# Attention with shared diagonal score blocks: pairs of diagonal blocks in 192 columns, and x loaded in quarters

## The chip, the cores and the metric

The kernel runs on one core of one Trainium2 chip. A core has a matrix engine (PE, with its weight loads shown apart as PEld), a vector engine (DVE), a scalar engine (ACT), GpSimd (POOL), a queue engine (SP) that here only issues DMAs, an on-chip memory (SBUF)[...]. The metric is device time in microseconds of one execution, as the median of several runs.

## The reference

For each of 32 images with 256 channels and 1024 positions, the input is normalised in groups of eight channels, projected to queries, keys and values of eight heads of 32 channels, and each position attends to the positions strictly before it. Position 0 has no such position and receives 0. The input is added to the result.

```python
xf = _gn(x).reshape(B, C, S)                    # 32 groups of 8 channels
q = jnp.einsum('oc,bcs->bos', q_w, xf) + q_b[None, :, None]
kv = jnp.einsum('oc,bcs->bos', kv_w, xf) + kv_b[None, :, None]
k, v = (kv[:, :EMBED_C], kv[:, EMBED_C:])       # then q, k, v to 8 heads
mask = jnp.tril(jnp.ones((S, S), dtype=x.dtype), -1)
scores = jnp.einsum('bhqd,bhkd->bhqk', q, k) / jnp.sqrt(dk)
attn = jax.nn.softmax(jnp.where(mask == 0, -10000.0, scores), axis=-1)
attn = jnp.where(mask == 0, 0.0, attn)
out = x + jnp.einsum('bhqk,bhkd->bhqd', attn, v)   # back to B, C, H, W
```

## The kernel before

All is float32. The 256 channels are two groups `g` of 128 partitions, each with four heads of 32 partitions; the 1024 positions are two halves `hf` of 512 queries and eight key blocks `kb` of 128. Scores are computed transposed, with keys on partitions and queries along the columns. Only the blocks on and below the diagonal are computed, 36 blocks of 128x128 for each head.

**Pieces and visits.** A `piece` is what one key block gives to one half of the queries: 512 columns, or 256 (a half piece). Pieces of which a part lies above the diagonal are filled up: the second diagonal key block of a half has 384 columns and takes the last 128 from the fourth. For each group there are six visits of one full and one half piece, and so twelve visits in a batch element (called a batch here). The list `visits` says which pieces are scored together, and `products` which are then multiplied by the values.

**A visit.** The main loop does, in this order for visit i: `scores(i)`; then what hangs on `at[i]` (one unit of the projections of the next batch, the issue of loads, `stack`, `invert`); then `values(i-1)`, the products of the visit before; then what hangs on `after[i]` (normalisation steps, `fold`, `sum_folded`, `finish`). [...] The places of the hooks within the twelve visits are the lists `PROJECT`, `PREPARE`, `SUMS` and `FINISH`.

- `scores` (L285): each product has 32 rows (one head) and 64 keys, so that four heads and two halves of a key block occupy different parts of the PE array. The half pieces of heads 2 and 3 come first, then the full piece of heads 0 to 3, then, after a wait on the semaphore `bank_free`, the half pieces of heads 0 and 1, which share their banks with those of heads 2 and 3. Three exponentials on ACT follow: two of the full piece (L348, tile `e`) and one of the half piece (L346, tile `eh`). A full float32 product stands in the trace as two passes.
- `mask` (L301): a select on POOL sets the part of diagonal blocks above the diagonal to 0, in place in `e` or `eh`.
- `values` (L373): products of 128 keys and 32 channels for each head, into one accumulator bank per half. At the last one ACT copies the bank to `num` (L386). An addition on DVE (L381) sums the exponentials of a half over its key blocks, into the tile of its first piece (tag `e0`).
- The denominators: `fold` adds the 128 partitions of that sum onto 32 by two accumulating DMAs from POOL's queue (L397, with a drain before the second one for n=1), `stack` moves them by SP, `sum_folded` (L410, L411), `invert` and two DMAs bring the inverses back as `rb`.
- `finish` (L483, L484): `num` times `rb`, plus the bias of v, plus x; then the output DMA.
- Normalisation of a later batch: `norm_channels` (statistics on DVE, L168), `norm_mean` (a product `pm` on PE, L158), `norm_deviation` (three small DVE steps `dev`, L186 to L188), `norm_variance` (a product `pv` on PE, which reads `dev`), `norm_rstd` (POOL), `norm_apply` (ACT, L224, tile `xn`). `pm` is at the end of visit 3 and `pv` at the end of visit 4 of the batch before.
- Projections (L158 through `product`): q and k in 512 columns, v in 256, from `xn`.
- `load` (L107): two DMAs of 512 KB for a batch, in visit 6.

In the last batch some of the key sums are made by PE (`sums`, L418) in place of the additions, and the inverses by DVE alone (`invert_here`).

Of the kernel before, what the change touches and what calls it, by code (L numbers as in the profile page):

```python
# [17 lines left out]
P = 128  # L18
# [10 lines left out]
WIDE = 64  # L29
# [3 lines left out]
def tile_norm_attention_residual(  # L33
# [65 lines left out]
    def unshifted():  # L99
# [3 lines left out]

        def load(b):
            live["x", b] = xpool.tile([P, NG, S], F32, tag="x", name=f"x_{b}")
            for g in range(NG):
                nc.sync.dma_start(out=live["x", b][:, g, :], in_=x_in[b, :, g, :])  # L107
# [16 lines left out]
        def load_weights():  # L124
            for n, w in enumerate((q_w, kv_w[0:C], kv_w[C : 2 * C])):
                live["wn", n] = epool.tile([P, 4, HALFBANK], F32, tag="eh", bufs=4, name=f"wn_{n}")[:, :NG, :C]
                nc.sync.dma_start(out=live["wn", n], in_=w.rearrange("(o p) c -> p o c", p=P))
            nc.sync.dma_start(out=qk_bias[:, 0, :], in_=q_b.rearrange("(g p) -> p g", p=P))
            nc.sync.dma_start(out=qk_bias[:, 1, :], in_=kv_b[0:C].rearrange("(g p) -> p g", p=P))
            nc.sync.dma_start(out=v_bias_col, in_=kv_b[C : 2 * C].rearrange("(g p) -> p g", p=P))  # L130
# [30 lines left out]


# [49 lines left out]
        def norm_apply(b, hf, g):  # L212

            if (hf, g) == (0, 0):
                live["xn", b] = work.tile([P, NG, S], F32, tag="xn", name=f"xn_{b}")
            cols = slice(hf * HALF, (hf + 1) * HALF)
            xn, xt = live["xn", b][:, g, cols], live["x", b][:, g, cols]
            rstd = live["rstd", b][:, g : g + 1]
            if (b, hf, g) == (0, 0, 1):
                nc.scalar.activation(xn, live["less_mean"], AF.Identity, scale=rstd)  # L220
            elif b == 0:
                nc.vector.tensor_scalar(xn, xt, live["minus_mean", b][:, g : g + 1], rstd, ALU.add, ALU.mult)
            else:
                nc.scalar.activation(xn, xt, AF.Identity, bias=live["shift", b][:, g : g + 1], scale=rstd)  # L224

        def project_qk(b, g, n, hf):
# [6 lines left out]
            for cc in range(NG):  # L233
                product(
                    pp, wT[:, cc, n * C + g * P : n * C + (g + 1) * P], live["xn", b][:, cc, cols],
# [6 lines left out]
        def project_v(b, n):  # L242
# [4 lines left out]
            pp = spare(f"ppv_{b}_{n}").rearrange("p (s c) -> p s c", c=C)  # L247
            for s in range(2):
                for cc in range(NG):
                    product(  # L250
                        pp[:, s, :], live["xn", b][:, cc, (2 * n + s) * P : (2 * n + s + 1) * P],
                        wT[:, cc, 2 * C : 3 * C], start=cc == 0, stop=cc == NG - 1,
                    )
# [12 lines left out]
        def piece(g, hf, k, part=None):  # L266
            d = k - hf * BPH
            if d == 1:

                blocks = [(k, slice(P, HALF), slice(P, HALF)), (k + 2, slice(0, P), slice(3 * P, HALF))]  # L270
            elif d == 2:
                blocks = [(k, slice(0, HALFBANK), slice(HALFBANK, HALF))]
            elif part is not None:
                blocks = [(k, slice(0, HALFBANK), slice(part * HALFBANK, (part + 1) * HALFBANK))]
            else:
                blocks = [(k, slice(0, HALF), slice(0, HALF))]
            return g, hf, k, part, tuple(blocks)

        def scores_of(pc, pair, j, n=0):

            b, (g, hf, k, part, blocks) = pc
            rows = slice(HD * j, HD * (j + 1))
            kb, cols, of = blocks[n]
            return [
                nc.tensor.matmul(  # L285
                    pair[c : c + WIDE, cols], lhsT=live["k", b, g][rows, kb * P + c : kb * P + c + WIDE],
                    rhs=live["q", b, g][rows, hf * HALF + of.start : hf * HALF + of.stop],
                    start=True, stop=True, skip_group_check=True,
                )
                for c in range(0, P, WIDE)  # L290
            ]

        def mask(pc, e, heads=slice(0, 4)):


            g, hf, k, part, blocks = pc
            if k < hf * BPH:
                return
            n = len(blocks)
            diagonal = e[:, heads, : n * P].rearrange("p j (n q) -> p j n q", q=P)  # L300
            nc.gpsimd.affine_select(  # L301
                out=diagonal, in_=diagonal, pattern=[[0, heads.stop - heads.start], [0, n], [1, P]],
                compare_op=ALU.is_gt, fill=0.0, base=0, channel_multiplier=-1,
            )
            if k == 0:
                nc.gpsimd.memset(e[0:1, heads, 0:1], 1.0)

        def scores(b, full, half):


            tag = "e0" if full[2] == 0 else "e"
            name = f"{b}_{full[0]}_{full[1]}_{full[2]}"
            e = epool.tile([P, 4, HALF], F32, tag=tag, bufs=4 if tag == "e0" else 3, name=f"{tag}_{name}")
            eh = epool.tile([P, 4, HALFBANK], F32, tag="eh", bufs=4, name=f"eh_{name}")
            pairs = [ps_s.tile([P, 2, HALF], F32, tag="sT", name=f"sT_{name}_{a}") for a in range(3)]
            short = pairs[2].rearrange("p bank (n q) -> p bank n q", n=2)
            last = b == B - 1 and full[:2] == (NG - 1, NH - 1) and half[2] == NB - 2
            short_of = lambda heads, n: [m for j in heads for m in scores_of((b, half), short[:, j % 2, n, :], j)]
            long_of = lambda heads, n: [scores_of((b, full), pairs[j // 2][:, j % 2, :], j, n) for j in heads]


            if not last:
                first = short_of((2, 3), 1)
                for n in range(len(full[4])):
                    long_of(range(4), n)
            else:

                long_of(range(4), 0)
                long_of((0, 1), 1)
                first = short_of((2, 3), 1)  # L330
                long_of((2, 3), 1)

            for ins in first:
                ins.then_inc(bank_free, 1)
                tc.no_tile_sem_insts.add(ins.ins.name)
            live["free"] = live.get("free", 0) + len(first)
# [3 lines left out]
            for j in range(2):  # L340
                for lo in scores_of((b, half), short[:, j, 0, :], j):
                    for ins in first:
                        tc.declare_no_dep(lo.ins, ins.ins, reason="the semaphore orders them")
            for a in range(3):
                if a == 2:
                    exp = nc.scalar.activation(eh.rearrange("p (n bank) q -> p bank n q", n=2), short, AF.Exp)  # L346
                else:
                    nc.scalar.activation(e[:, 2 * a : 2 * a + 2, :], pairs[a], AF.Exp)  # L348
# [6 lines left out]
            for heads in (range(2), range(2, 4)) if last else (range(4),):  # L355
                mask(full, e, slice(heads.start, heads.stop))
            mask(half, eh)
            live["e", b, full], live["e", b, half] = e, eh

        def values(b, pc, summed=True):  # L360
            g, hf, k, part, blocks = pc
            first, last = k == 0, k == hf * BPH + (1 if hf == 0 else 2)
            e = live.pop(("e", b, pc))
            if not summed:
                live["e", pc] = e
            if first:
                live["acc"] = ps_o.tile([P, HALF], F32, tag="acc", name=f"acc_{b}_{g}_{hf}")
                live["sum", b, g, hf] = e
            acc = live["acc"]
            for kb, cols, of in blocks:  # L370
                for j in range(4):
# [3 lines left out]
                        rhs=e[:, j, cols], start=first, stop=last, skip_group_check=True,  # L375
                    )
                if not summed:
                    continue
                if not first:
                    total = live["sum", b, g, hf]  # L380
                    nc.vector.tensor_add(total[:, :, of], total[:, :, of], e[:, :, cols])  # L381
            if last and (b, g, hf) == (B - 1, NG - 1, NH - 1):
                live["num", b, NH * g + hf] = acc
            elif last:
                num = work.tile([P, HALF], F32, tag="num", bufs=8, name=f"num_{b}_{g}_{hf}")
                nc.scalar.copy(num, acc)  # L386
                live["num", b, NH * g + hf] = num
# [28 lines left out]
        def sum_keys(pd, e, cols, of, start=True, stop=True):  # L416
            for j in range(4):
                nc.tensor.matmul(  # L418
                    pd[HD * j : HD * (j + 1), of], lhsT=pick, rhs=e[:, j, cols],
# [3 lines left out]
        def sums(n, pcs, more=True):  # L423
# [4 lines left out]
            for k, e in enumerate(pcs):  # L428
                if e is None:
                    e, blocks = live.pop(("sum", B - 1, *divmod(n, NH))), ((None, slice(0, HALF), slice(0, HALF)),)  # L430
                else:
                    e, blocks = live.pop(("e", e)) if ("e", e) in live else live["e", B - 1, e], e[4]
                for kb, cols, of in blocks:
# [371 lines left out]
```

## Time and profile before

| | us |
|---|---|
| median of 3 runs (1822.09 to 1822.13) | 1822.12 |
| the profiled execution | 1821.87 |
| its span | 1820.1 |
| PE busy | 1807.9 |
| DVE busy | 1655.6 |
| ACT busy | 1480.0 |
| POOL busy | 798.9 |

The profile is one execution. Its span runs from the first to the last instruction; the profiled execution's own time lies 1.8 us above it. Busy time is the union of an engine's instructions, so overlapping matmuls are counted once; it says how much an engine had to do, and not which wait decided. For that the timeline is read stage by stage. Lines such as L285 are those of the kernel before.

### The profile page before, as it was taken

The page shows a single profiled execution, that of the slowest core. Times are in us where ns is not written, and L with a number is a line of the kernel's source. Part 1 is how long each engine was busy: PE and PEld are TensorE (multiplying, and loading weights), DVE is VectorE, ACT ScalarE, POOL GpSimd, SP SyncE. Part 2 cuts the span into 40 slices and gives each one's busy share as a digit, 9 for nine tenths or more (in the row PEclk, how much of TensorE's full clock was granted, in tenths as well). Part 3 has the DMA queues.
Part 4 walks back from the last instruction along what each step waited for, and adds up shares of the span by engine and source line. Part 5 has one row for each costly group of instructions (what it writes and reads, how often), then busy time and mean ns, then how long its engine had stood idle before and what let it go on. Part 6 is the DMA issues. An engine that isn't in the chain of part 4 may idle for free. (4 is left out here: it accounts for less than half of the span.)

```text
span 1820.1 us, 68098 instructions
## 1 busy us (share of the span) xinstructions
PE 1807.9 (99%) x30388; PEld 837.4 (46%) x30388; DVE 1655.6 (91%) x1762; ACT 1480.0 (81%) x1860; POOL 798.9 (44%) x774
## 2 busy tenths in 40 slices
PE   9999999999999999999999999999999999999997
PEld 5444444444444444444444444444444444444443
DVE  4799999999999999999999999999999999999988
ACT  6888878888888888788887888877888878888885
POOL 1444544535435445344354353443444544435532
PEclk9999999999999999999999999999999999999999
DMA  3457676676776766767767667676667676676662
GB/s 123 71 98 137 134 150 113 133 148 125 147 127 125 143 128 137 148 121 133 142 129 147 116 135 150 124 141 136 123 137 136 134 152 115 129 152 124 124 124 73
DMA packets 77836, 235.91 MB, mean 130 GB/s; under 512 B 20320, under 2 KB 21344, under 8 KB 61664
## 3 DMA queue, kind: packets, MB, share of 16 engines
q0 software_dynamic: 15872, 97.53, 40.1%
q1 hardware_dynamic: 61664, 133.96, 26.4%
q8 instruction: 239, 3.92, 0.9%
q14 instruction: 61, 0.50, 0.1%
HBM read 66.85 MB, written 34.57 MB: 56 GB/s over the span
## 5 line engine op out<-in xcount | busy, mean ns | idle before, releaser
L348 ACT ACTIVATE e<-sT 128x1024 f32<-128x1024 f32 x768 | 745.2, 1022 | 269.3 <-PE sT L285 214.5
L381 DVE TENSOR_TENSOR e<-e,e 128x1536 f32<-128x1536 f32 x376 | 632.5, 1682 | 17.7
L381 DVE TENSOR_TENSOR e<-e,eh 128x1024 f32<-128x1024 f32 x380 | 524.2, 1394 | 112.3 <-PE acc L373 92.8
L301 POOL TENSOR_SCALAR_AFFINE_SELECT e<-e 128x512 f32<-128x512 f32 (+1 forms) x257 | 381.9, 1486 | 549.6 <-ACT e L348 546.4
L285 PE MATMUL sT<-q,k 32*64 32x256 f32 (+3 forms) x14336 | 601.3, 447 | 0.2
L158 PE MATMUL pp<-xn,wT 128*32 128x512 f32 x4096 | 492.4, 598 | 0.1
L285 PEld LDWEIGHTS sT<-q,k 32*64 32x64 f32 x14336 | 353.3, 130 | 212.9 <-ACT eh L346 64.7
L373 PE MATMUL acc<-e,v 128*32 128x512 f32 (+2 forms) x4096 | 400.8, 486 | 0.0
L346 ACT ACTIVATE eh<-sT 128x1024 f32<-128x1024 f32 x384 | 395.6, 1030 | 0.0
L397 POOL DMA_DIRECT2D e<-e x248 | 202.0, 824 | 399.5 <-DMA e<-e 305.3
L158 PE MATMUL ppv<-wT,xn 128*32 128x256 f32 x4096 | 247.5, 382 | 0.0
L373 PEld LDWEIGHTS acc<-e,v 128*32 128x32 f32 x4096 | 133.1, 110 | 223.1 <-issue 192.1
L373 PE MATMUL acc<-eh,v 128*32 128x256 f32 x3072 | 224.6, 379 | 0.0
L158 PEld LDWEIGHTS pp<-xn,wT 128*32 128x32 f32 x4096 | 107.5, 109 | 237.2 <-issue 228.9
L373 PEld LDWEIGHTS acc<-eh,v 128*32 128x32 f32 x3072 | 98.8, 110 | 164.0 <-issue 153.0
L158 PEld LDWEIGHTS ppv<-wT,xn 128*32 128x32 f32 x4096 | 120.3, 109 | 110.8 <-issue 44.7
L301 POOL TENSOR_SCALAR_AFFINE_SELECT eh<-eh 128x512 f32<-128x512 f32 x128 | 166.7, 1302 | 0.6 <-ACT eh L346 0.2
L224 ACT ACTIVATE xn<-x,shift,rstd 128x512 f32<-128x512 f32 x124 | 103.1, 831 | 0.0
L484 DVE SCALAR_TENSOR_TENSOR rb<-rb,v_bias_col,x 128x512 f32<-128x512 f32 x124 | 94.0, 758 | 4.4
L238 ACT ACTIVATE k<-pp,qk_bias 128x512 f32<-128x512 f32 x128 | 89.8, 702 | 2.3 <-PE pp L158 1.2
L238 ACT ACTIVATE q<-pp,qk_bias 128x512 f32<-128x512 f32 x128 | 89.9, 702 | 1.0 <-PE pp L158 1.0
L410 DVE STREAM_TRANSPOSE turned<-folded 128x512 f32<-128x512 f32 x124 | 87.6, 706 | 2.2
(70 smaller groups left out, 665.8 us busy)
## 6 DMA issues: line engine op xcount, KB each, us to landing
e<-e POOLq DMA_DIRECT2D x124, 512.0 KB, 6.8
x<-in_x_dram SPq DMA_DIRECT2D x64, 512.0 KB, 6.3
e<-e POOLq DMA_DIRECT2D x124, 256.0 KB, 4.6
folded<-e SPq DMA_DIRECT2D x124, 256.0 KB, 3.9
rb<-inverses SPq DMA_DIRECT2D x124, 256.0 KB, 8.0
out_dram<-rb SPq DMA_DIRECT2D x124, 256.0 KB, 4.7
inverses<-inv_turned SPq DMA_DIRECT2D x31, 32.0 KB, 1.7
out_dram<-rb_last SPq DMA_DIRECT2D x3, 256.0 KB, 2.5
```

The lines of the kernel that those rows point to most:

```text
L158: nc.tensor.matmul(out[part], lhsT=lhsT[:, part], rhs=rhs, start=start, stop=stop, skip_group_check=True)
L224: nc.scalar.activation(xn, xt, AF.Identity, bias=live["shift", b][:, g : g + 1], scale=rstd)
L238: nc.scalar.activation(live[key][:, cols], pp, AF.Identity, bias=qk_bias[:, n, g : g + 1], scale=(SCALE, 1.0)[n],)
L285: nc.tensor.matmul(pair[c : c + WIDE, cols], lhsT=live["k", b, g][rows, kb * P + c : kb * P + c + WIDE], rhs=live["q", b, g][rows, hf * HA ...
L301: nc.gpsimd.affine_select(out=diagonal, in_=diagonal, pattern=[[0, heads.stop - heads.start], [0, n], [1, P]], compare_op=ALU.is_gt, fill= ...
L346: exp = nc.scalar.activation(eh.rearrange("p (n bank) q -> p bank n q", n=2), short, AF.Exp)
L348: nc.scalar.activation(e[:, 2 * a : 2 * a + 2, :], pairs[a], AF.Exp)
L373: nc.tensor.matmul(acc[HD * j : HD * (j + 1), of], lhsT=live["v", b][:, kb, h * HD : (h + 1) * HD], rhs=e[:, j, cols], start=first, stop=l ...
L381: nc.vector.tensor_add(total[:, :, of], total[:, :, of], e[:, :, cols])
L397: nc.gpsimd.dma_start(out=total[:rows], in_=total[rows : 2 * rows], accum_op=ALU.add)
L410: nc.vector.transpose(turned, live["folded", b][:, j, :])
L484: nc.vector.scalar_tensor_tensor(rb, rb, v_bias_col[:, g : g + 1], xt[:, g, cols], ALU.add, ALU.add)
```

## The change

Two diagonal blocks 2j and 2j+1 were scored in full, 256 columns of 128 keys. Half of each is above the diagonal. The change writes both into 192 columns. It first orders the tokens of each pair of blocks so that the odd block runs backwards (`blocks` with `turned`, when x is normalised into `xn`; `finish` turns the result back). Then the upper 64 keys of the odd block need only its first 64 queries, and so on, and the two blocks' triangles fit beside each other: for the lower 64 partitions 64 columns of the odd block and 128 of the even one, for the upper 64 partitions 128 of the odd and 64 of the even one. `mask` makes the two square blocks of them, each by a select from the raw exponentials in `eh` into a new tile, `diagonal` (kind "D"), one for each half.

The lists of pieces are replaced by tables: `VISITS` (what is scored), `PRODUCTS` (which columns of which tile are multiplied by which values), `ADDS` (which tiles are added into which) and `SUMMED` (the last batch's sums on PE). Four of six visits of a group have a pair beside a long piece of 512 columns (or 384 + 128); two have a half piece of 256. The long pieces now contain only blocks below the diagonal, and need no mask. The sum of the first half is kept in its diagonal tile, that of the second half in the long tile of visit 2. The loads of x become four of 256 KB, in visits 4 to 7. The buffers for `e` go from 3 to 4, for `eh` from 4 to 3, and `xn` is kept in halves with 3 buffers.

```diff
         def norm_apply(b, hf, g):
...
-                nc.scalar.activation(xn, xt, AF.Identity, bias=live["shift", b][:, g : g + 1], scale=rstd)
+            for s in range(2):
+                to, of = blocks(xn, s), blocks(xt, s, s == 1)
+                if b == 0:
+                    nc.vector.tensor_scalar(to, of, live["minus_mean", b][:, g : g + 1], rstd, ALU.add, ALU.mult)
+                else:
+                    nc.scalar.activation(to, of, AF.Identity, bias=live["shift", b][:, g : g + 1], scale=rstd)
...
+        def blocks(tokens, s, turned=False):
+            of = tokens.rearrange("p (n s t) -> p n s t", s=2, t=P)[:, :, s, :]
+            return of[:, :, ::-1] if turned else of
...
+        def pair(j, at):
+            even, odd = 2 * j, 2 * j + 1
+            c0, c1, c2, c3 = (at + n * KEYS for n in range(4))
+            return at, 3 * KEYS, [
+                [
+                    (0, even, even * P, P, slice(c1, c3)),
+                    (0, odd, odd * P, KEYS, slice(c0, c1)),
+                ],
+                [
+                    (KEYS, odd, odd * P, P, slice(c0, c2)),
+                    (KEYS, even, even * P + KEYS, KEYS, slice(c2, c3)),
+                ],
+            ]
...
+        def mask(b, g, raw, j):
+            hf, place = j // 2, (2 * j % 4) * P
+            if ("e", b, g, "D", hf) not in live:
+                live["e", b, g, "D", hf] = epool.tile(
+                    [P, 4, HALF], F32, tag=("e0", "e")[hf], bufs=4, name=f"diagonal_{b}_{g}_{hf}"
+                )
+            square = live["e", b, g, "D", hf]
+            for s in range(2):
+                nc.gpsimd.affine_select(
+                    out=square[:, :, place + s * P : place + (s + 1) * P],
+                    in_=raw[:, :, (1 - s) * KEYS : (3 - s) * KEYS],
+                    pattern=[[0, 4], [(1, -1)[s], P]], compare_op=ALU.is_gt, fill=0.0, base=0,
+                    channel_multiplier=(-1, 1)[s],
+                )
...
         def scores(b, v):
...
+            rest = [lambda: long_of((2, 3), 1)] if len(longs) > 1 else []
+            first = short_of((2, 3))
+            for n in range(len(longs) - 1, -1, -1):
+                long_of((0, 1), n)
+            long_of((2, 3), 0)
...
+            made = short_of((0, 1), *rest if i in PAIRS else ())
...
+        def add_keys(b, v):
+            g, i = divmod(v, len(VISITS))
+            for to, at in ADDS[i]:
+                to = tile_of(b, g, to)
+                nc.vector.tensor_add(to, to, tile_of(b, g, at))
...
         def finish(b, n, within=slice(0, HALF)):
...
-            nc.vector.tensor_mul(rb, num[:, within], rb)
-            nc.vector.scalar_tensor_tensor(rb, rb, v_bias_col[:, g : g + 1], xt[:, g, cols], ALU.add, ALU.add)
+            num = num[:, within]
+            nc.vector.tensor_mul(num, num, rb)
+            for s in range(2):
+                nc.vector.scalar_tensor_tensor(
+                    blocks(rb, s), blocks(num, s, s == 1), v_bias_col[:, g : g + 1], blocks(xt[:, g, cols], s),
+                    ALU.add, ALU.add,
+                )
...
+        VISITS = [
+            ([full(0, P, 3 * P, 0), full(2, 3 * P, P, 3 * P)], [pair(0, 0)]),
+            ([full(1, 2 * P, 4 * P, 0)], [pair(1, 0)]),
+            ([full(0, 4 * P, 4 * P, 0)], [full(1, 6 * P, 2 * P, 0)]),
+            ([full(2, 4 * P, 4 * P, 0)], [pair(3, 0)]),
+            ([full(4, 5 * P, 3 * P, 0), full(6, 7 * P, P, 3 * P)], [full(5, 6 * P, 2 * P, 0)]),
+            ([full(3, 4 * P, 4 * P, 0)], [pair(2, 0)]),
+        ]
+        N, TOTAL = NG * len(VISITS), 2
+        PAIRS = {0: 0, 1: 1, 3: 3, 5: 2}
...
+            (0, [
+                (("L", 0, Q(0, 3)), 0, Q(1, 4)), (("L", 0, Q(3, 4)), 2, Q(3, 4)),
+                (("D", 0, Q(0, 1)), 0, Q(0, 1)), (("D", 0, Q(1, 2)), 1, Q(1, 2)),
+            ]),
+            (0, [(("L", 1, Q(0, 2)), 1, Q(2, 4)), (("D", 0, Q(2, 3)), 2, Q(2, 3)), (("D", 0, Q(3, 4)), 3, Q(3, 4))]),
...
+        ADDS = [
+            [(("L", 0, Q(2, 3)), ("L", 0, Q(3, 4)))],
+            [(("D", 0, Q(1, 4)), ("L", 0, Q(0, 3))), (("D", 0, Q(2, 4)), ("L", 1, Q(0, 2)))],
+            [(("L", 2, Q(0, 2)), ("L", 1, Q(2, 4))), (("L", 2, Q(2, 4)), ("H", 2, Q(0, 2)))],
+            [(("L", 2, Q(0, 4)), ("L", 3, Q(0, 4)))],
+            [
+                (("L", 2, Q(1, 4)), ("L", 4, Q(0, 3))), (("L", 2, Q(3, 4)), ("L", 4, Q(3, 4))),
+                (("L", 2, Q(2, 4)), ("H", 4, Q(0, 2))),
+            ],
+            [(("L", 2, Q(0, 4)), ("D", 1, Q(0, 4))), (("L", 2, Q(0, 4)), ("L", 5, Q(0, 4)))],
+        ]
...
-                    when(max(first - 2 * N + 6, 0), lambda b=b: load(b))
+                    for n in range(NG * NH):
+                        cols = slice(n % NH * HALF, (n % NH + 1) * HALF)
+                        when(max(first - 2 * N + 4 + n, 0), lambda b=b, n=n, cols=cols: load_part(b, n // NH, cols))
```

## The prediction

> **What bounds the kernel now.** I read the page first, for busy shares; then the timeline of one steady batch, PE and DVE apart, because a share of 99% says nothing of where it would give; then the groups by form for durations, and the waits.
>
> The page, part 1:
>
> ```profile
> PE 1807.9 (99%) x30388; PEld 837.4 (46%) x30388; DVE 1655.6 (91%) x1762; ACT 1480.0 (81%) x1860; POOL 798.9 (44%) x774
> ```
>
> TensorE never rests; DVE has 9% left, most of it at the start. A batch is twelve visits (0 to 11). The timeline of PE in visits 4 and 5 (start, length; records overlap, so stages are read start to start):
>
> ```profile
> 654.17 1.93 PE L158 MATMUL ppv<-wT,xn 128*32 128x256 f32 x32
> 655.92 1.04 PE L373 MATMUL acc<-e,v 128*32 128x512 f32 x8
> 656.78 0.61 PE L373 MATMUL acc<-eh,v 128*32 128x256 f32 x8
> 657.27 0.24 PE L158 MATMUL pv<-dev,avg 128*32 128x2 f32 x8
> ...
> 657.44 1.59 PE L285 MATMUL sT<-q,k 32*64 32x256 f32 x48
> 658.96 1.92 PE L158 MATMUL pp<-xn,wT 128*32 128x512 f32 x16
> 660.70 1.04 PE L373 MATMUL acc<-e,v 128*32 128x512 f32 x8
> 661.56 0.61 PE L373 MATMUL acc<-eh,v 128*32 128x256 f32 x8
> 662.10 1.55 PE L285 MATMUL sT<-q,k 32*64 32x256 f32 x32
> 663.58 1.93 PE L158 MATMUL pp<-xn,wT 128*32 128x512 f32 x16
> ```
>
> A visit is scores (662.10 to 663.58, 1.48 us; 1.52 where the long piece is split 384+128), projection (1.74), values (1.40 for 768 columns). Within a score stage the single records put the two passes of a 512-column product 427 ns apart and of a 128-column one 107: 0.83 ns per column and pass, 1.667 per column. So 768 columns are 1.28 of the 1.48 us. DVE over visits 3 and 4:
>
> ```profile
> 649.67 0.69 DVE L483 TENSOR_TENSOR rb<-num,rb 128x512 f32<-128x512 f32 x1
> 650.39 0.75 DVE L484 SCALAR_TENSOR_TENSOR rb<-rb,v_bias_col,x 128x512 f32<-128x512 f32 x1
> 651.18 0.15 DVE L486 COPY rb<-x 128x1 f32<-128x1 f32 x1
> 651.99 2.36 DVE L381 TENSOR_TENSOR e<-e,eh 128x1024 f32<-128x1024 f32 x2 [0.66 <-PE acc L373]
> 654.27 0.68 DVE L483 TENSOR_TENSOR rb<-num,rb 128x512 f32<-128x512 f32 x1
> ...
> 655.66 0.15 DVE L186 TENSOR_TENSOR dev<-mv,mean 128x2 f32<-128x2 f32 x1
> 655.85 0.16 DVE L187 TENSOR_TENSOR dev<-dev 128x2 f32<-128x2 f32 x1
> 656.04 0.54 DVE L188 TENSOR_TENSOR dev<-dev,mv 128x2 f32<-128x2 f32 x1
> ```
>
> The small `dev` ends at 656.58 and the product `pv` on PE that reads it starts at 657.27: 0.69 us to spare, once per batch. That is the narrowest place between the two busiest engines.
>
> Groups by form (busy, mean ns) and one wait:
>
> ```profile
> L381 DVE TENSOR_TENSOR e<-e,eh 128x1024 f32<-128x1024 f32 x380 | 524.2, 1394 | 112.3 <-PE acc L373 92.8 <-POOL e L301 1.6 <-DVE e L381 0.5
> L301 POOL TENSOR_SCALAR_AFFINE_SELECT eh<-eh 128x512 f32<-128x512 f32 x128 | 166.7, 1302 | 0.6 <-ACT eh L346 0.2
> L484 DVE SCALAR_TENSOR_TENSOR rb<-rb,v_bias_col,x 128x512 f32<-128x512 f32 x124 | 94.0, 758 | 4.4
> ```
>
> ```profile
> PEld sT L285 <- ACT eh L346: 64.7, 189, 0.7
> ```
>
> The add of 1024 takes 1.22 us alone, 1.51 or 1.94 beside a select; a select 0.67 alone, 0.97 or 1.65 beside an add. The last row says that weight loads of a score stage often come just after the exponential `eh`: in steady visits it ends 0.16 to 1.0 us before the next stage.
>
> [...] the two passes of the 2-column `pm` start 29 ns apart. [...] in split stages products for heads 0,1 start 0.19 us before older ones for heads 2,3. [...] a score stage has 196 ns beyond its stream, a projection 34. [...]
>
> **Part by part.** *Scores.* Each half has 6 visits; four of them get a 192-column pair in place of 256 columns: 64 x 1.667 = 107 ns less, on the path. 4 x 64 (batch, group) x 107 = 27.3 us saved. The 384+128 split moves from visits 1 and 5 to 0 and 4: nothing. Passes of 64 columns: two per pair and row group. Cost below: 0[...]; above: 29 ns each[...], 15 us in all. I take 4 ns, 2 us.
>
> The pair also puts 8 products ahead of the first long one for heads 0,1, where 4 stood. It must be pulled past 12 queued passes; the trace shows 8. If it is not, the long product starts up to 0.25 us late and the saving is gone; kept for the range.
>
> *Values.* Columns stay 4608 per group; 19 products for 14. A stage of 384+128+256 takes 1.408 against 1.403: 5 x 4 ns x 64 = 1.3 us.
>
> *Exponentials.* 256 of the `eh` have 768 elements: 1030 - 213 = 0.82 us, ACT only. The normalisation `xn` is written in two strided halves, one read backwards: 831 to 2 x 618, overlapped 0.12, so +0.29 us in four visits of a batch. It runs beside `eh`'s gain and before the long product is ready at 1.18 us; in visit 8, the tightest, I find `eh` 20 ns later of 157. Nothing on the path; 0.1 us x 31 above.
>
> *Masks.* Selects of e or eh in place (8 of 512, 4 of 1024 elements a batch) become 16 of 512 from the raw scores into a new tile. POOL has room (44%). They end about one us into the next visit; the values that need them come last, at 3.7 or later. They queue with the fold DMAs, whose sums come no later than before, and the drain before the second fold of n=1, which now stands behind visit 9's mask: its issue slides within visit 10, and the stack on SP is at 11.
>
> *Loads.* Four of 256 KB in visits 4 to 7 for two of 512 KB in visit 6; SP passes them ahead of the stack in 5. The statistics read x in visit 9. Nothing. Batch 0's normalisation on DVE, also halved, runs once: 0.2 us. Buffers: e 4 for 3, eh 3 for 4, xn 3 halves: each reuse is two visits or more behind its last reader; nothing.
>
> *DVE.* Adds: 11 instructions for 12, 3584 columns both, alone 16.4 us for 16.6 a group. `finish` has two additions of 256 (485 ns, shown by the last batch) for one of 512 (752): +0.13 to 0.22 us each, four a batch.
>
> **The new wait.** The first half's sum is now kept in the diagonal tile, whose last blocks PE reads in visit 1's values. So the add of visit 1 (384 and 256) waits for all of that stage; before, 128x1536 went ahead with no such wait. Behind it on DVE stand finish 2, visit 2's adds, finish 3, `dev`; `pv` on PE waits for `dev`, and the next scores stand behind `pv`. Worked out: before, visit 2's add starts 1.165 us after its values (0.853 stream + 0.312). So the gate is 1.476 + 1.741 + 0.853 + 0.316 = 4.386 into visit 2, which lasts 4.197: 0.19 into visit 3. Then 1.716 + 0.104 + 1.217 - 0.083 (adds), 1.75 (finish 2), 2 x 1.14 (adds), 1.52 (finish 3), 0.54 (`dev`, its last step 0.16 alone; no select falls there now): 9.24. Visit 3 lasts 5.098 - 0.107, so `dev` ends 4.25 into visit 4. `pv` is wanted at 4.57 to 4.61. But visit 3's pair sends two selects at 3.9, amid these two-input instructions; a select between two adds cost DVE 0.30 to 0.36 in visits 0 and 1, up to 0.5 where one instruction follows without a gap. Two: 0.75, and 0.1 for the semaphore: 5.1, a stall of 0.45 us, in 28 batches: 12.6 us. Ends: 0 (selects fall elsewhere), and 1.2 us or 34 (DVE also late at the gate).
>
> **The end.** The last chain is DVE without a break from 1781; eight `finish` steps of +0.2: 2 us. PE's own sums of the last batch grow by 384 columns (0.6 us) beside that chain.
>
> Sum: -27.3 + 2 + 1.3 + 0.2 + 12.6 + 2 = -9.2. The profiled execution took 1821.87 (span 1820.1 and 1.8 around), the median 1822.12: 1812.7.
>
> **Rivals.**
> 1. `dev` is in time: -9.2 - 12.6 = -22, 1800. For it: 0.3 us to spare without selects. Against: those land at 3.9.
> 2. DVE becomes the bound: slower. Place: the add gated at visit 3. DVE is busy 52.10 of 55.81 us per batch (windows of twelve visits); the new period without stalls would be 54.9. Four more selects' worth[...] (0.36 each, 1.4) and finish 0.5 to 0.9 make 54.4; another 1.3 us per batch, and the stall is 1.2 us or more: -22 + 34 = +12, 1834. It decides from a stall of 0.8 us.
> 3. The pair isn't overlapped[...]: 256 x 0.1 given back, 1812.7 + 26 = 1839.
>
> **Chances.** Forecast 0.45 (1804 to 1821), rival 1 0.22, rival 2 0.20, rival 3 0.10, the rest 0.03. Faster by over 0.2% (3.6 us, what a measurement here can tell): rival 1 and three quarters of the forecast, 0.55. Within: 0.13. Slower: 0.32. Range 1797 to 1834: it takes in rival 1 and most of rival 2. The forecast's own is 1804 to 1821.
>
> **What would show it.** Score stages with a pair at 1.37 to 1.40; if 1.48, the saving failed. `pv` waiting on `dev` L197 in the waits, 0.45 us a time, and DVE's add of 1536 waiting on `acc` at the start of visit 3; no such wait means rival 1. DVE busy over 97% in the windows means rival 2. I am wrong altogether if PE waits for POOL's masks or for ACT's `eh`.

## The result, and the profile after

| | before | after |
|---|---|---|
| median, us | 1822.11 | 1835.19 (1833.93 to 1838.15) |
| the profiled execution, us | 1821.87 | 1834.49 |
| its span, us | 1820.1 | 1832.8 |

The ratio is 1.0075, with a 95% interval of 1.0058 to 1.0093. The forecast was 1812.7: the sign was wrong, and the time lies 1 us beyond the range. The profiled execution is 12.6 us longer, where the sum of the prediction had it 9.2 shorter, so 21.8 us are to be explained.

Two lines of the page of the kernel after: the first with busy time, share and instructions of each engine, and one of the DMA queues (transfers, MB, share), that of the engines' instructions.

```profile
PE 1800.6 (98%) x37036; PEld 958.2 (52%) x37036; DVE 1642.0 (90%) x1832; ACT 1456.2 (79%) x1985; POOL 842.1 (46%) x901
...
q8 instruction: 291, 4.77, 1.1%
```

The same queue on the page of the kernel before:

```profile
q8 instruction: 239, 3.92, 0.9%
```

PE is busy 7.3 us less in a span that is 12.7 longer: work went, and waits came. It also executes 6648 more weight loads and as many more matmuls, and the instruction queue has 52 transfers more. DVE is not the bound; it is busy 51.81 of 55.83 us in the windows of a batch.

A share does not place a wait. So I measured each stage of PE from its first matmul to the first of the next stage, over 28 batches (2 to 29). Medians in us; the last column is the mean of what visits lasted beyond their usual length, summed over a batch:

```
            scores in visit: 0     1     2     3     4     5    values in visit 4   stops a batch
before                     1.476 1.518 1.476 1.476 1.476 1.518        1.341             0.06
after                      1.496 1.403 1.476 1.404 1.481 1.403        1.865             0.38
```

Visits 6 to 11 repeat the scores of 0 to 5. The stage of values in visit 4 is taken up to the first matmul of `pv`. Over a batch the scores gain 0.553 us, this one values stage loses 0.524, PE stops for 0.32 more, and the other values stages cost 0.05. That makes +0.34 a batch, and the measured batch went from 55.871 to 56.208.

**Visit 4.** The timeline of the kernel after, visits 3 to 5 (start, length; in brackets the idle time before and what ended it):

```profile
650.50 3.09 DVE L427 TENSOR_TENSOR diagonal<-diagonal,e 128x1536 f32<-128x1536 f32 x2 [0.27 <-issue]
...
658.57 1.04 PE L409 MATMUL acc<-e,v 128*32 128x512 f32 x8
...
659.25 0.60 ACT L266 COPY v<-ppv 128x512 f32<-128x512 f32 x1
...
660.00 0.64 PE L409 MATMUL acc<-diagonal,v 128*32 128x128 f32 x16 [0.39 <-ACT v L266]
660.07 0.16 DVE L197 TENSOR_TENSOR dev<-dev,mv 128x2 f32<-128x2 f32 x1
...
660.43 0.25 PE L162 MATMUL pv<-dev,avg 128*32 128x2 f32 x8
...
660.61 1.47 PE L302 MATMUL sT<-q,k 32*64 32x128 f32 x48
...
662.01 1.92 PE L162 MATMUL pp<-xn,wT 128*32 128x512 f32 x16
```

And its waits (total, times, longest):

```profile
PE acc L409 <- ACT v L266: 12.5, 32, 0.4
```

After the 512 columns of visit 3's values, PE stands before the diagonal products until ACT has copied `v` (659.25 + 0.60, and 0.12 to the first weight load). These products multiply v of key blocks 6 and 7, which the projection of the same visit has just made. Before, the values of visit 3 used blocks 2 and 3, and blocks 6 and 7 were first wanted by those of visit 5. No step of the prediction had this wait. `dev` ends at 660.23, 4.90 us into the visit, and `pv` starts 0.20 later: the predicted wait is there too, but hidden behind the other.

**Visit 0.** The timeline of PE in batch 12:

```profile
692.74 1.36 PE L302 MATMUL sT<-q,k 32*64 32x128 f32 x49
695.92 0.44 PE L302 MATMUL sT<-q,k 32*64 32x128 f32 x15 [1.82 <-issue]
696.30 1.06 PE L162 MATMUL pp<-xn,wT 128*32 128x512 f32 x8
```

Within a score stage nothing starts for 2.09 us, and no semaphore is named. Stops of over 0.1 us are in 12 of 28 batches, all in visit 0. The trace has each transfer of the instruction queue; all have 16,384 bytes. Times in us around four of the stops, and the one of the kernel before:

```
                 transfer before ended   this one began   ended     PE goes on
after, batch 2          121.82               130.82       132.28     133.70
after, batch 10         569.67               579.67       580.80     582.21
after, batch 12         682.63               693.35       694.48     695.92
after, batch 24        1357.48              1366.76      1368.12    1369.66
before, batch 6         341.27               353.17       354.52     355.94
```

In all twelve stops PE goes on 1.3 to 1.6 us after such a transfer has ended, and always at a record whose number among PE's (its waits counted) is the same modulo 256. There are 252 such places in the 28 batches, one for each transfer in order, and PE passes none of them sooner than 1.30 us after its transfer has ended. I read this as PE having used up its instructions at the stops. The counts fit: 291 transfers for 74,072 loads and matmuls are 255 for each. The 256 records between two such places are called a block below.

That they all stand in visit 0 has a second reason. A batch has 2307 of these records, nine blocks and three, so in each of the 28 batches a block ends at nearly the same place of visit 0, just behind visits 10 and 11, in which the DMA engines are busy 98 and 99%. Before, a batch had 1892, 7.4 blocks: in 15 batches a block ended in visit 0, and PE stopped at one of them. After, it stopped at 12 of 28.

### The profile page after: what moved, and what is told of

Same layout as the page of the kernel before. It is cut to its first block, busy times and chain, and to the rows that moved or that the text cites. A ratio compares the mean times of both kernels' runs of the same rounds, so it can differ in the third digit from the quotient of the medians.

```text
span 1832.8 us, 81736 instructions
## 1 busy us (share of the span) xinstructions
PE 1800.6 (98%) x37036; PEld 958.2 (52%) x37036; DVE 1642.0 (90%) x1832; ACT 1456.2 (79%) x1985; POOL 842.1 (46%) x901
## 4 chain that ended last, share of the span: by engine, by line
PE 92%; ACT 6%; issue 1%; DVE 1%; DMA 0%; POOL 0%
PE sT L302 30%; PE pp L162 26%; PE acc L409 26%; PE ppv L162 10%; ACT e L384 3%; ACT eh L380 2%; ACT v L266 1%; PE pd L461 0%; DMA x<-in_x_dram 0%; PE pv L162 0%; DVE st L177 0%; PE pm L162 0%; POOL diagonal L330 0%; DVE rb_last L526 0%; DVE rb_last L514 0%
## 5 line engine op out<-in xcount | busy, mean ns | idle before, releaser
L330 POOL TENSOR_SCALAR_AFFINE_SELECT diagonal<-eh 128x512 f32<-128x512 f32 x512 | 541.6, 1081 | 777.9 <-ACT eh L380 777.8
L302 PE MATMUL sT<-q,k 32*64 32x128 f32 (+2 forms) x18432 | 587.7, 372 | 4.7 <-issue 4.4
L427 DVE TENSOR_TENSOR e<-e,e 128x1024 f32<-128x1024 f32 x315 | 541.9, 1720 | 19.5 <-ACT v L266 3.2
L409 PE MATMUL acc<-e,v 128*32 128x384 f32 (+3 forms) x4608 | 402.0, 450 | 0.0
L380 ACT ACTIVATE eh<-sT 128x768 f32<-128x768 f32 (+1 forms) x384 | 341.0, 888 | 0.0
L427 DVE TENSOR_TENSOR diagonal<-diagonal,e 128x1536 f32<-128x1536 f32 x126 | 188.0, 1492 | 25.7 <-PE acc L409 10.6
L427 DVE TENSOR_TENSOR e<-e,eh 128x1024 f32<-128x1024 f32 x127 | 171.5, 1351 | 6.9 <-ACT q L249 0.5
L409 PE MATMUL acc<-diagonal,v 128*32 128x128 f32 x4096 | 160.4, 273 | 12.5 <-ACT v L266 12.5
L427 DVE TENSOR_TENSOR e<-e,diagonal 128x2048 f32<-128x2048 f32 x62 | 142.1, 2292 | 24.1 <-POOL diagonal L330 20.7
L235 ACT ACTIVATE xn<-x,shift,rstd 128x256 f32<-128x256 f32 x248 | 137.2, 613 | 0.0
```

Of the source, the lines that this page charges most:

```text
L235: nc.scalar.activation(to, of, AF.Identity, bias=live["shift", b][:, g : g + 1], scale=rstd)
L302: return nc.tensor.matmul(bank[c : c + KEYS, cols], lhsT=live["k", b, g][rows, kb * P + c : kb * P + c + KEYS], rhs=live["q", b, g][rows, ...
L330: nc.gpsimd.affine_select(out=square[:, :, place + s * P : place + (s + 1) * P], in_=raw[:, :, (1 - s) * KEYS : (3 - s) * KEYS], pattern=[ ...
L409: nc.tensor.matmul(acc[HD * j : HD * (j + 1), of], lhsT=live["v", b][:, kb, h * HD : (h + 1) * HD], rhs=e[:, j, :], start=first, stop=last ...
L427: nc.vector.tensor_add(to, to, tile_of(b, g, at))
```

## The experiments

Medians are of each run's own executions; ratios are to executions of the kernel before that were timed beside them. Stage lengths and stops are those of one profiled execution.

### Which wait holds visit 4

`e_v` exchanges the last two units of the v projection, so that blocks 6 and 7 are made in visit 3:

```diff
-            return qk[0] + v[:1] + qk[1][:1] + v[1:2] + qk[1][1:] + qk[2] + v[2:] + qk[3]
+            return qk[0] + v[:1] + qk[1][:1] + v[1:2] + qk[1][1:] + qk[2] + v[3:] + v[2:3] + qk[3]
```

> The changed kernel with the third and fourth unit of the v projection exchanged: the one that makes v of blocks 6 and 7 runs in visit 3 and that of blocks 4 and 5 in visit 4. In the changed kernel PE stands before the diagonal products of visit 3 (in the values stage of visit 4) until ACT has copied v of blocks 6 and 7, and this stage lasts 1.865 us in place of 1.35. Theory A (two waits, one behind the other, of nearly one length): the wait for v goes, but pv on PE then waits for dev, which DVE finishes 4.90 us into visit 4 whatever PE does, so the stage stays at 1.8 to 1.87 us in 30 batches, only the first and last batch (without pv) lose 0.5 us each, and the time is 1834. Theory B (dev would be in time): the stage falls to 1.35 us, 32 x 0.52 = 16.6 us less, 1818.

`e_dev` puts `norm_mean` and `norm_deviation` first in their hook, ahead of `finish`:

```diff
+            early = [lambda: norm_mean(b), lambda: norm_deviation(b)]
...
+                elif f in early:
+                    after.setdefault(n, []).insert(early.index(f), f)
```

> The changed kernel with the three small dev steps (and the product pm) ahead of the fourth finish on DVE in place of behind it, so that dev is ready some 1.5 us earlier, about 3.4 us into visit 4. Theory A (two waits of nearly one length): v still holds the diagonal products until 4.67 us into visit 4, so pv starts no earlier and the time stays at 1834 to 1835. Theory C (the prediction's: pv waits for dev alone): the values stage of visit 4 falls from 1.865 to 1.35 us in 30 batches, 15.5 us less, 1819.

`e_v_dev` is both.

> Both edits together: v of blocks 6 and 7 a visit earlier, and dev ahead of the fourth finish. Theory A (two waits of nearly one length): only now the values stage of visit 4 falls from 1.865 to 1.35 us, 30 x 0.52 us + 2 x 0.6 = 16.7 us less than the changed kernel's 1835: 1818. Theories B and C (one wait alone): the same time as with that one edit.

| | values in visit 4, us | median, us | ratio to before, 95% |
|---|---|---|---|
| after | 1.865 | 1835.19 | 1.0075 (1.0058 to 1.0093) |
| e_v | 1.813 | 1826.85 | 1.0025 (1.0018 to 1.0033) |
| e_dev | 1.865 | 1830.03 | 1.0034 (1.0021 to 1.0047) |
| e_v_dev | 1.340 | 1815.07 | 0.9956 (0.9942 to 0.9970) |

The timeline of `e_v`, visit 4:

```profile
714.37 0.62 PE L409 MATMUL acc<-diagonal,v 128*32 128x128 f32 x16
...
715.02 0.16 DVE L197 TENSOR_TENSOR dev<-dev,mv 128x2 f32<-128x2 f32 x1
...
715.33 0.24 PE L162 MATMUL pv<-dev,avg 128*32 128x2 f32 x8 [0.34 <-DVE dev L197]
```

The timeline of PE in `e_dev`, visit 4:

```profile
717.46 0.65 PE L409 MATMUL acc<-diagonal,v 128*32 128x128 f32 x16 [0.39 <-ACT v L266]
717.89 0.25 PE L162 MATMUL pv<-dev,avg 128*32 128x2 f32 x8
```

With v early, PE runs through to `pv` and waits there for `dev`; with `dev` early it waits for v as before. Either wait alone keeps nine tenths or all of the 0.52 us, and only both edits free it. That is theory A by the stage lengths. The times of the single edits came lower than A said, by 7 and 4 us. Of the 7 of `e_v`, 2 are fewer stops in visit 0 (0.31 us a batch for 0.38); no run shows where the rest comes from. The profiled executions, 1829.2 and 1833.7, lie nearer to A than the medians, and executions of `e_v` go from 1824.7 to 1834.3. `e_v_dev` beats the kernel before.

### What the pair costs the scores

`e_order` lets only the 128-column products of heads 2 and 3 stand ahead of the long ones:

```diff
-            first = short_of((2, 3))
-            for n in range(len(longs) - 1, -1, -1):
-                long_of((0, 1), n)
+            ahead = lambda: [long_of((0, 1), n) for n in range(len(longs) - 1, -1, -1)]
+            first = short_of((2, 3), *(ahead,) if i in PAIRS else ())
+            if i not in PAIRS:
+                ahead()
             long_of((2, 3), 0)
```

> The changed kernel with another order of score products in the visits with a pair: of heads 2 and 3 only the four products of 128 columns stand ahead of the long products of heads 0 and 1, and their products of 64 columns come behind these. Theory W (the eight products ahead delay the long ones: these start 53 ns into the stage, 27 ns in the kernel before, where four stood ahead): the pair stages beside 512 columns fall from 1.403 to about 1.376 us and those beside 384 + 128 from 1.496 to about 1.47, 256 x 27 ns = 7 us less: 1828. Theory L (the loss is in the weight loads under the 64-column products): stages stay at 1.40 and 1.50, 1835.

It took 1935.39 us, ratio 1.0615 (1.0602 to 1.0629): a miss for both theories. PE's timeline of `e_order`, visit 1:

```profile
677.96 1.93 PE L302 MATMUL sT<-q,k 32*64 32x128 f32 x48
679.82 0.64 PE L162 MATMUL pp<-xn,wT 128*32 128x512 f32 x4
```

The stage lasts 1.86 us in place of 1.40. Its single records have the long products 26 ns into the stage, as theory W said, 53 in the kernel after. But the last products, which wait on `bank_free`, start at 1.372 where they did at 0.962. The first of the 64-column products that count `bank_free` up ends at 0.54 in both. In the kernel after, the wait is over 0.18 us later; here, where the long products of heads 0 and 1 stand ahead of them in the program, it is over 0.83 later, 0.26 after those long ones end. No run isolates what holds them, so the cause of the 0.83 us stays open. The order of the change is the better one. Its price, by the records, is 27 ns at the start of a pair stage and some 7 for the short passes.

### Why PE runs out of instructions

`e_fold` takes the mask of visit 9 out of the way of the two folds behind it:

```diff
-            if i in PAIRS:
+            if v == 9 and b < B - 1:
+                live["late_mask"] = lambda: mask(b, g, eh, PAIRS[i])
+            elif i in PAIRS:
                 mask(b, g, eh, PAIRS[i])
...
                 for f in after.pop(i, ()):
                     f()
+                live.pop("late_mask", lambda: None)()
```

> The changed kernel with the mask of visit 9 written behind the two folds of that visit in POOL's order, so that these (256 and 512 KB by accumulating DMAs) are issued before the four transfers of inverses (256 KB each) instead of amid them; in the changed kernel the DMA engines are busy 98 and 99% in visits 10 and 11, in the kernel before 91 and 92%. In the changed kernel the score stage of visit 0 lasts 1.869 us on average in place of 1.496: PE stands still in it in 11 of 28 batches without waiting on a semaphore, and goes on 1.3 to 1.5 us after a transfer of 16 KB of its instructions has ended. Theory D (the folds, which slid by a visit, hold up these transfers): the stage falls to 1.50 us on average, 10 us less: 1825. Theory I (PE uses up its instructions faster, 2315 in a batch in place of 1899 or so, and the transfers were held up as long before): the stops stay, at least half of them, 1830 to 1836.

`b_instr` adds instructions to the kernel before:

```diff
-            short_of = lambda heads, n: [m for j in heads for m in scores_of((b, half), short[:, j % 2, n, :], j)]
+            short_of = lambda heads, n: [
+                m for cut in ((0, 192), (192, 256)) for j in heads for m in scores_of((b, half), short[:, j % 2, n, :], j, 0, cut)
+            ]
```

> The kernel before, with each half piece of 256 score columns made by two products of 192 and 64 columns: the same columns, transfers and sums, but 384 PE instructions more in a batch. The split itself costs each of 384 score stages some 30 to 40 ns (eight products ahead of the long ones, shorter passes), 12 to 15 us. Theory I (the count of PE instructions makes PE stop for its instructions): stops appear in the score stage of visit 0 or near it in at least 8 of 28 batches, 5 to 12 us more in sum, 1840 to 1850. Theory D (the folds that slid): no more stops than the one of 0.75 us of the kernel before, 1834 to 1837.

`b_instr` took 1869.58 us, 1.0281 (1.0257 to 1.0304). Its instruction queue on the page, and PE's timeline in visit 11 of batch 11:

```profile
q8 instruction: 287, 4.70, 1.0%
```

```profile
700.47 1.25 PE L158 MATMUL ppv<-wT,xn 128*32 128x256 f32 x16
703.71 0.41 PE L158 MATMUL ppv<-wT,xn 128*32 128x256 f32 x2 [1.99 <-issue]
```

A batch lost 1.06 us in visits 0, 5 and 11, where the kernel before lost 0.06, with the same data moved. A batch has 2276 records here, so that the ends of the blocks move through the visits as they did before; a fixed place in visit 0 is not needed for stops. More PE instructions were enough here: theory I, though the stops cost some 30 us where I had put 5 to 12. The split cost 34 ns in a stage of 512 + 256 columns (1.476 to 1.510), as the pair did, and 98 beside 384 + 128, more than I had put.

`e_fold` took 1884.87 us, 1.0355 (1.0337 to 1.0372). The folds did come earlier, and a batch lost about 2.0 us in visit 0 in place of 0.38. Theory D is out, but so is a theory in which transfers do not matter. From here on the base is `e_v_dev`. `e_spread` is to send two of the four transfers of the inverses later:

> The kernel with v a visit earlier and dev ahead of the fourth finish (1815), and in it two of the four transfers that bring the inverses (256 KB each, at the end of visit 9) sent four visits later, in visit 0, where the DMA engines are half idle; they are wanted by the first finish in visit 2. PE's stops in visit 0 came to 0.23 us a batch in the score stage and 0.03 in the projection. Theory Q (PE's instructions wait in the DMA engines behind the inverses and the folds of visits 10 and 11): with half of the inverses out of the way the 16 KB transfers are held up less, and at least two thirds of the stops go, 5 us or more: 1808 to 1810. Theory N (only the number of instructions decides): 1815, stops as before. Worse than 1817 would mean that the transfers collide with others in visit 0, or that finish waits.

```diff
-            for h in range(4):
+            send(b, (0, 1))
+
+        def send(b, heads):
+            spread = live["spread", b]
+            for h in heads:
                 nc.sync.dma_start(
...
+                    when(v + (4 if late else 6), lambda b=b: send(b, (2, 3)))
```

It took 1817.47, 0.9975 (0.9967 to 0.9982), and says nothing on the theories: SP's order is not written by hand, and the timeline of SP still has all four transfers within 2.02 us at the end of visit 9. Visit 0, where two were to go, has a DMA share of 0.57 in the kernel after (mean of 28 batches). In `e_send` ACT issues the two later ones:

```diff
-                nc.sync.dma_start(
+                (nc.sync if h < 2 else nc.scalar).dma_start(
```

> As the run that was to send two of the four transfers of the inverses later, but with these two issued from ACT's queue behind the exponentials of visit 0, where the order is written by hand; SP's is not, and there all four still left together at the end of visit 9. Base: the kernel with v a visit earlier and dev ahead of the fourth finish (1815 to 1817), whose stops in visit 0 are 0.26 us a batch. Theory Q (PE's instructions wait in the DMA engines behind the inverses and folds of visits 10 and 11): fewer and shorter stops, at least two thirds less, 5 us: 1810 to 1812. Theory N (only the number of instructions decides): 1815 to 1817.

`e_late` moves the folds of the third sum by two visits (`SUMS = (3, 7, 11, 13)` for `(3, 7, 9, 13)`).

> The same base, with the first fold of the third sum (512 KB, issued in visit 10 amid the transfers of the inverses) and what follows it two visits later, in visit 11 behind its mask. The run that issued the folds earlier, amid the inverses, made the stops longer (1.7 us a batch in place of 0.37). Theory Q (PE's instructions wait in the DMA engines behind what is queued there): with this fold out of visits 10 and 11 the interval between the transfers of instructions there falls under 8.5 us (8.2 to 10.8 in the base), and the stops in visit 0 go or move to visits 1 and 2, where the fold now is: 1808 to 1814. Theory N: 1815 to 1817.

`e_send3` sends three of the four from ACT.

> As the run with two transfers of the inverses sent from ACT's queue in visit 0 (1812), with three sent there and one at the end of visit 9. Theory Q (PE's instructions wait in the DMA engines behind what is queued there): the transfers of instructions in visit 11 come sooner than 8 us after the ones before them in most batches, and the stops in visit 0 fall from 0.15 us a batch to under 0.1: 1809 to 1812; if stops move to visit 1 or 2, where 768 KB now go, it gains nothing, 1812 to 1815. It is not slower than 1816 by either; finish waiting on the inverses in visit 2 would be the reason if it is.

Loss in us a batch beyond the usual length, by visit, and DMA share of visits 10 and 11 (a packet's whole time is counted where it begins):

```
             visit 0   visit 1   visit 4   DMA 10  DMA 11   median us   ratio to before, 95%
e_v_dev       0.26      0.00      0.00      0.97    1.00     1815.07    0.9956 (0.9942 to 0.9970)
e_send        0.15      0.02      0.00      0.79    0.90     1811.97    0.9937 (0.9924 to 0.9950)
e_late        0.01      0.00      0.34      0.96    0.51     1821.63    0.9999 (0.9989 to 1.0009)
e_send3       0.11      0.16      0.01      0.54    0.89     1817.91    0.9978 (0.9969 to 0.9987)
```

Less traffic in visits 10 and 11, fewer stops in visit 0, each time, as theory Q had it, though `e_send` lost two fifths of its stops and not two thirds; what a transfer of instructions waits for in the DMA engines, no trace shows. Where the transfers stayed as they were, visit 0 lost 0.26, 0.28 (`e_spread`) and 0.39 us (`e_xwhole`). The clearest is `e_late`: it emptied visit 0 and got its stops back in visit 4, two visits past where I had put them, with 0.06 more in visit 8, and gained nothing. `e_send3` came out above the 1816 that I had put as its limit. The reason that I had named is there, `finish` waits for the inverses for 8.4 us in all, but what PE loses it loses in visit 1. This run shows what else the transfers did to ACT. Its timeline, visits 0 and 1 (ACTq is ACT's queue as it issues):

```profile
412.96 2.85 ACTq L503 DMA_DIRECT2D rb<-inverses  x1
...
415.85 0.96 ACTq L503 DMA_DIRECT2D rb<-inverses  x1
...
416.86 0.69 ACT L249 ACTIVATE k<-pp,qk_bias 128x512 f32<-128x512 f32 x1 [2.32 <-PE sT L302]
...
417.60 1.49 PE L162 MATMUL pp<-xn,wT 128*32 128x512 f32 x12 [0.80 <-ACT k L249]
```

ACT issues one transfer for 2.85 us, the copy of `k` stands behind the next one, and PE's projection behind that. `e_send`, with two such transfers, has the lowest median of the study. It is clearly faster than the kernel before; that it is faster than `e_v_dev` is not shown by the times, as the intervals overlap and `e_spread`, whose transfers leave as in `e_v_dev`, lies 2.4 us from it.

`e_xwhole` undoes the loads in quarters, on `e_v_dev`:

> The same kernel (1815) with x loaded as before, by two transfers of 512 KB in visit 6 in place of four of 256 KB in visits 4 to 7. The prediction's cost of the loads, nothing: 1815 within 2 us. If the quarters hold up PE's instructions or the stack on SP less than whole loads do, it is slower, by 3 us or more, with stops in visits 5 to 8 that the other has not.

It took 1815.62, 0.9960 (0.9947 to 0.9973): no difference.

## The prediction, point by point

Two steps failed. The score term was mis-sized: it gained 17.7 us where the sum had 25.3. And what the additional PE instructions cost beyond the columns that they stream was put at nothing: PE stood without instructions for some 10 us more. A third, the values, had a right number over a wait that it had missed.

The terms of the sum beside what the profiles hold, in us over the whole run (a batch's figure times 32, unless said):

| term | predicted | measured |
|---|---|---|
| scores, with their 64-column passes | -25.3 | -17.7 |
| values | +1.3 | +1.6 |
| waits in visit 4 | +12.6 | +16.9 (30 x 0.524, and 0.6 in each of two batches without `pv`) |
| the end (batch 31 and what follows), batch 0 | +2.2 | +2.8 |
| PE without instructions | none | +10 (0.32 more a batch) |

The measured terms come to 13.6 where the profiled execution has 12.6: the first two batches and the last are not quite like the 28 in between, and the last is also in the row of the end.

1. *Scores: right in direction, mis-sized by 7.6.* I took 4 ns as the price of the 64-column passes, an estimate of mine that no run had shown; in the kernel after, the two passes of such a product start 56 ns apart, 3 more than 64 columns take at 0.83. A pair stage beside 512 columns lasts 1.403 where the sum had 1.37. The missing term there is the delay of the long product of heads 0 and 1, which I kept for the range only: 27 ns more, not 0.25 us. It starts 53 ns into the stage, ahead of twelve older passes, and rival 3 did not come. One beside 384 + 128 lasts 1.496 where the sum had 1.41; of these 85 ns the same delay and the short passes account for 34, and what makes the rest stays open. The reordered stage without a pair gained 37 ns (1.518 to 1.481), which I had at nothing.
2. *Values: the number was right, and the step failed.* I counted columns and the readiness of the masks; PE hardly waits for masks (0.3 us in the values of the whole run). I did not go through what else the diagonal products read. Their v is made in the same visit, and that is a new wait of 0.52 us. It is luck for the sum that this wait and the predicted one are of nearly one length and lie at the same time: the row of visit 4 came out near its number, 16.9 for 12.6.
3. *The new wait on `dev`: right, and out of sight.* The gate was put 0.19 us into visit 3, at 650.50, where the add starts; `dev` was put 5.1 us into visit 4 with the semaphore and ended at 4.90; the stall was put at 0.45 (by its own terms, 5.1 less 4.57 to 4.61, it is about 0.5; its 0.1 for the semaphore is 0.15 in `e_v`, from the end of `dev` at 715.18 to `pv` at 715.33) and is 0.47 where v is early (1.813 less 1.340). In the kernel after it shows nowhere, as the wait for v ends at the same time.
4. *ACT, masks, loads, buffers at nothing: right.* An `eh` of 768 elements takes 0.82 us, as put, and a half of `xn` 613 ns where 618 was put. PE waits for `eh` 14.3 us in all where it was 64.7, and hardly for masks; the loads are nothing by `e_xwhole`.
5. *The folds.* I saw that the fold of n=1 would slide within visit 10 and costed only its landing. It was no loss: moved back it cost 50 us.
6. *The step that was missing.* The 13,296 additional PE instructions were priced by the columns they stream. In visits 9 to 0 PE goes through 800 instructions in 18.8 us in place of 640 in 19.0. By the trace a transfer begins at the earliest 256 + 46 records ahead of its place, so by an estimate from these figures it has about the time of 256 instructions, 6.0 us for 7.6, less 1.1 of its own and 1.4 until PE goes on: 3.5 us to spare in place of 5.1, beside DMA engines that are busy 98 and 99% in visits 10 and 11. Transfers began about as late before (in the table at most 11.90 us after the last one had ended, for 10.72), but PE came to the end of its block later. The kernel before had a stop there too, one of 0.75 us. The instruction queue on its page was the hint, and I did not read it.

Rival 2 named 1834, near the result, but not by its reason: DVE is at 93% of a batch in place of over 97%, and the stall is under 0.8 us.

## What to carry to other kernels

When a table says which block is multiplied when, follow every operand of the new order to the instruction that makes it, not only the one that the change is about: here two waits of nearly equal length behind one another looked like one, and taking away either gave 0.05 us or nothing of 0.52. In a kernel bound by PE, count its instructions as well as its columns: here 800 of them in 18.8 us of visits 9 to 0, beside DMA engines busy 98 and 99% in visits 10 and 11, left too little reserve, and an idle stretch of PE ended by "issue" 1.3 to 1.6 us after an instruction transfer was the sign. Moving large data transfers helped or harmed PE, which never reads their data: visit 0 lost 0.15 us a batch in place of 0.26 in `e_send`, and 2.0 in place of 0.38 in `e_fold`.

## What the hardware did that I had not expected

In `e_fold` a stop cost more than its length. PE stood still for 3.2 us in visit 0 of batch 13; the timeline of PE behind it:

```profile
771.86 0.45 PE L302 MATMUL sT<-q,k 32*64 32x128 f32 x16 [2.90 <-issue]
772.23 3.49 PE L162 MATMUL pp<-xn,wT 128*32 128x512 f32 x16
```

And the windows of 2 us (busy time and instructions of PE, PEld, DVE, ACT and POOL, then the granted clock, DMA share and GB/s):

```profile
772.00:774.00 2.00, 2.00 (x28) 0.67 (x29) 1.90 (x2) 1.63 (x2) 0.00 (x0) 0.61 0.70 74
774.00:776.00 2.00, 2.00 (x14) 0.43 (x8) 1.53 (x1) 0.32 (x2) 1.83 (x2) 0.54 0.32 70
776.00:778.00 2.00, 2.00 (x56) 1.17 (x52) 0.00 (x0) 1.05 (x2) 0.66 (x3) 1.00 0.30 61
```

The projection takes 3.49 us in place of 1.92, at a granted clock of 0.54 to 0.61, and by 776 all is as before. The clock records of `e_fold` have six such stretches before its end, each behind a stop, at 0.5 and 3.41 us long; the two windows hold 2 x (0.39 + 0.46) / 0.5 = 3.4 us of one. The length of a stop alone does not tell: one of 1.98 us (batch 8) was followed by slow passes, one of 2.31 (batch 15) and one of 2.73 (batch 24) were not, and behind the longest of the kernel after, 2.09 us, the granted clock stayed at 1.00. What decides it, these runs do not show.
